# A hybrid block on one core: some of VectorE's products and sums given to GpSimd, with new ranks for the planner

## The chip, the core and the metric

The kernel runs on one NeuronCore of a Trainium2 chip. The time is the device time of one execution in microseconds (us); less is better. Engines are named as the profile names them: PE is TensorE (matmuls; PEld its weight loads), DVE is VectorE, ACT is ScalarE, POOL is GpSimd, SP is SyncE, which only issues DMAs. Each engine works through its own list of instructions in the order in which they stand; they wait for each other through semaphores.

## The reference

The input is x, 8 sequences of 256 tokens with 128 features, all in float32. Four layers are added to it one after the other, each on a layernorm of x:

```python
x = x + mamba(_layernorm(x))       # "m": a selective state space layer
x = x + moe(_layernorm(x))         # "p": 8 experts, two for each token
x = x + attention(_layernorm(x))   # "a": gated, with squared relu for the softmax
x = x + moe(_layernorm(x))         # "r": the same experts and weights again
```

In the first layer a projection gives 256 channels and a gate; a convolution over 4 tokens and a silu give h; delta = softplus(ts @ dt_w + dt_b); and for each of 256 channels and 16 states a recurrence runs over the 256 tokens: new = exp(A * delta) * old + delta * B * h, y = sum over the states of new * C, plus D * h. In an expert layer each token has a weight w_e for each of 8 experts (two are not zero), and the output is the sum over e of w_e * ((x @ w_up[e]) * silu(x @ w_gate[e])) @ w_down[e], with 352 inner features an expert.

## The kernel before

**Groups and lanes.** The 8 sequences are cut into four groups g of two, so a group has 512 tokens, which are the columns of nearly every tile (128 x 512). A group goes through lanes of work, each a Python generator: `prelude` (s: norm, projection, convolution, softplus), `recurrence` (m), `gating` (g), `ending` (f), `tail` (t), and `rest` (r: expert layer p, attention, expert layer r). `feeder` loads B and C rows and has ACT make the decays; `adder` issues the DMAs that sum the states' shares.

**Who sets the order.** A planner in the kernel, `Board` (L32 to L86), writes the order down when the program is built. Each lane offers its next operation with a cost in us; the planner takes the one that can start first by its own clock (`pick`, L73), with `RANKS` (L150) where several of one engine are near, and issues it. `SWITCH` is what it takes an ACT table load to cost. An engine's list is thus fixed before the kernel runs, and the chip follows it whether the costs were right or not. Where the planner thinks that PE will be idle for long before an operation, it puts dummy matmuls of 128 x 128 into its list (`fill`, L321 to L325, in `do` at L59 to L64), one for each 0.23 us of idle time as it sees it. They compute nothing that is used.

**The recurrence** (L724). 16 states by two channel halves are done in 16 steps for each group, 64 in all. A step is three instructions on DVE over 128 x 1024: a product (L744), a scan (L749) and a product (L753). All their operands are in SBUF. Then POOL issues a DMA (L716) that adds the step's result into an accumulator tile; five tiles `st0` to `st4` serve all.

**The softplus** (L607 to L635) is taken apart as max(v, 0) + log(1 + exp(-|v|)) with a correction. For each half c of the channels DVE subtracts the correction from dl (L624), later adds the logarithm to dl (L632), and multiplies dl by h to give du (L633). Decays are made from dl, the recurrence's first product reads du. In group 0 the two halves are separate steps; in later groups the correction (L622) is one instruction over both.

**An expert layer** (L945). The 8 x 352 inner features are 22 tiles of 128. For each tile: a gate product on PE (`gp`, L487), a silu on ACT (`sg`, L960), an up product on PE (`up`, L986, or L993 in four parts where a tile holds the end of one expert and the start of the next), a product on DVE (`it`, L1000, which reads `up` from PSUM), and two tiles later a down product on PE (`dn`, L1006). The token's weight is put into the input of `up`: a row of w_e is spread over the partitions by a DMA (`fetched`, L966) into a tile wb, and wb is multiplied by xT in place (`weighted`, L974 to L977, on DVE, both operands in SBUF). Of wb three tiles are held for each key, and expert e+2 is weighted when expert e has its last tile, two to three tiles ahead of its use. For layers in `SOON` the first expert's tile comes another way (L927 to L942).

**On POOL before the change** stand the L716 issues, the powers of the norms (L415), and the biases added to x (L494, 128 x 512), eight in all.

Of the kernel before, what the change touches and what calls it, by code (L numbers as in the profile page):

```python
# [10 lines left out]
ALU = mybir.AluOpType  # L11
# [20 lines left out]
class Board:  # L32
# [1 line left out]


    SWITCH = 1.3
    PATIENCE, LONG = 0, 0
    FILL = 0.23

    def given(self, op):  # L40
# [55 lines left out]
def kernel(  # L96
# [27 lines left out]
    nc = tc.nc  # L124
# [23 lines left out]
    BEHIND = 2  # L148

    RANKS = {  # L150
        "s": [0, 4, 4, 1.5], "m": [1.5, 2, 3, 3.5],
        "g": [4, 0, 3.5, 2], "t": [0, 3.5, 3.5, 0.5],
        "r": [2, 0.5, 2.5, 0.5], "f": [2.5, 1.5, 4, 0.5], "w": [0, 0, 0.3, 0], "feeder": 5, "adder": 0,
    }
    SOON = ("p0", "p1", "r0", "p3", "r3")
    SPLIT = ()
    ENDS = 2
    assert E * F % P == 0 and all(cut >= P or cut % CG == 0 for _, cut in OWNER)
# [36 lines left out]
    for name, src in (  # L195
# [10 lines left out]
        n = src.shape[0]  # L206
# [75 lines left out]
    def ring(pool, shape, tag, name, bufs=1):  # L282

        held = rings.setdefault((pool.name, tag), [])
        free = held[-bufs].used if len(held) >= bufs else 0.0
        h = Held(pool.tile(shape, FP, tag=tag, name=name, bufs=bufs), free)
        held.append(h)
        return h
# [40 lines left out]
    def dve(us, out, ins, issue):  # L329
        return Op("DVE", us, out, ins, issue, lag=0.06)  # L330
# [4 lines left out]
    def pool(us, out, ins, issue):  # L335
        return Op("POOL", us, out, ins, issue, lag=0.06)

    def load(us, out, ins, issue, queue="SP", take=0.1):
        return Op(queue, take, out, ins, issue, lag=us)

    def mm(n):
        return 0.005 + 0.00167 * n
# [4 lines left out]
    def dve_us(n):  # L347
        return 0.08 + 0.0012 * n
# [22 lines left out]
    for k in range(K):  # L371
# [6 lines left out]
    PARTS = [  # L378
        [(b, b + 1) for b in range(n)] if g in SPLIT else [(0, n)] for g, n in enumerate(SIZES)
    ]  # L380
# [137 lines left out]
    def prelude(g):  # L518

        GB = SIZES[g]  # L520
        G = GB * T
# [3 lines left out]
        xT = ring(norm, [P, G], "xTm", f"xT_m{g}")  # L525
# [4 lines left out]
        h = [ring(mam, [P, G], f"h{c}", f"h_{g}_{c}", bufs=2) for c in range(NI)]  # L530
# [52 lines left out]
        shut(ps)  # L583
        bc = Held(dram.tile([2 * N, G], FP, tag="bc", name=f"bc_{g}"))
        yield load(2.4, [bc], [ww], lambda: nc.sync.dma_start(bc.ap, xpj[R:XW, :]))

        dl = [ring(mam, [P, G], f"dl{c}", f"dl_{g}_{c}", bufs=2) for c in range(NI)]
# [22 lines left out]
        du = [ring(mam, [P, G], f"du{c}", f"du_{g}_{c}", bufs=2) for c in range(NI)]  # L612
# [6 lines left out]
        for (a, b), e, w in zip(parts, exs, wws):  # L619

            def lost():
                nc.vector.scalar_tensor_tensor(e.ap, w.ap, 1.0, e.ap, ALU.subtract, ALU.subtract)  # L622
                for c in range(a, b):
                    nc.vector.tensor_sub(dl[c].ap, dl[c].ap, e.ap[:, c - a, :])  # L624

            yield dve(2 * (b - a) * dve_us(G), [e] + dl[a:b], [w], lost)
        for (a, b), w in zip(parts, wws):
            yield act(act_us((b - a) * G), [w], [], lambda: nc.scalar.activation(w.ap, w.ap, AF.Ln, bias=zero), EXP)
        for (a, b), w in zip(parts, wws):
            for c in range(a, b):  # L630
                def step():
                    nc.vector.tensor_add(dl[c].ap, dl[c].ap, w.ap[:, c - a, :])  # L632
                    nc.vector.tensor_mul(du[c].ap, dl[c].ap, h[c].ap)  # L633

                yield dve(2 * dve_us(G), [dl[c], du[c]], [w, h[c]], step)  # L635
        if g > 0:

            for c in range(NI):
# [27 lines left out]
    def feeder():  # L666

        for g in range(NG):
# [6 lines left out]
            for q in range(N // NC):  # L675
# [4 lines left out]
                for tag, r0 in (("bt", q * NC), ("ct", N + q * NC)):  # L680
                    t = ring(scan, [P, NC, G], tag, f"{tag}_{g}_{q}", bufs=2)
                    yield load(4.0, [t], [bc], lambda: nc.sync.dma_start(
                        t.ap, bc.ap[r0 : r0 + NC, :].partition_broadcast(P)
                    ))
                    rows_at.append(t)
# [23 lines left out]
    def adder():  # L709

        while len(done & {f"f{g}" for g in range(NG)}) < NG:
            if not sums:
                yield None
                continue
            g, us, acc, st, into, of = sums.pop(0)
            yield load(us, [acc], [st], lambda: nc.gpsimd.dma_start(  # L716
                into, of, accum_op=ALU.add
            ), "POOL", 0.9)
            st.used = max(st.used, acc.ready)
            landed[g] = landed.get(g, 0) + 1  # L720
            if st is not acc:
                st.open = False
# [98 lines left out]
    def parted(g, tile):  # L821
        return tile, [Held(tile.ap[:, tokens(g, p)], tile.used) for p in range(len(PARTS[g]))]

    def whole(tile, parts):

        tile.ready = max(h.ready for h in parts)
        tile.used = max(h.used for h in parts)
        return tile
# [15 lines left out]
    def led_in(g, which, key, p, shared):  # L844
# [31 lines left out]
        if "we" not in shared:  # L876
# [8 lines left out]
            ]  # L885
            if f"{which}{g}" in SOON:
                shared["wb"] = parted(g, ring(
# [38 lines left out]

        if f"{which}{g}" not in SOON:  # L927
            return
# [16 lines left out]
    def moe(g, which, key, shared, ends):  # L945

        nm = f"{which}{g}"
        NT = SIZES[g] * TT
        G = NT * P
        xT, we = (whole(*shared[k]) for k in ("xT", "we"))  # L950
# [5 lines left out]
        def gate(i):  # L956
            gp = bank([P, G], f"gp_{nm}_{i}")
            yield pe(mm(G), [gp], [xT], product(gp.ap, [(wg_sb[:, i * P : (i + 1) * P], xT.ap)]))
            sg = ring(ffn, [P, G], f"sg{key}", f"sg_{nm}_{i}", bufs=SG)
            yield act(act_us(G), [sg], [gp], lambda: nc.scalar.activation(  # L960
                sg.ap, gp.ap, AF.Silu, bias=zero
            ), SILU)
            shut(gp)
            sgs[i] = sg
# [9 lines left out]
        def weighted(e):  # L974

            wb = wx[e]
            yield dve(dve_us(G), [wb], [xT], lambda: nc.vector.tensor_mul(wb.ap, wb.ap, xT.ap))  # L977

        def up(i, cols_of, sg, wa, wn, it, width):
# [49 lines left out]
        for i in range(LEAD):  # L1029
            yield from gate(i)  # L1030
        ahead = which + str(g) in SOON
        if not ahead:
# [3 lines left out]
        if not ahead:  # L1036
            yield from weighted(0)
        yield from weighted(1)

        dns = [  # L1040
# [4 lines left out]
        for i in range(NK - ENDS):  # L1045
            if i + LEAD < NK:
                yield from gate(i + LEAD)
            e, cut = OWNER[i]
            its[i] = tile_of(i)
            yield from up(i, everything, sgs.pop(i), wx[e], wx.get(e + 1), its[i], G)  # L1050
            if cut <= P:

                if e + WB < E:
                    yield from fetched(e + WB)
                if e + 2 < E:
                    yield from weighted(e + 2)
            if i >= BEHIND:
                it = its.pop(i - BEHIND)
                for p, dn in enumerate(dns):
                    yield from down(i - BEHIND, dn, it, tokens(g, p))  # L1060
# [179 lines left out]
    for g in range(NG):  # L1240
        waiting.append(Lane((RANKS["s"][g], g), prelude(g), [f"g{g - 1}"] * (g > 0) + [f"t{g - 2}"] * (g > 1)))
        waiting[-1].name = f"s{g}"
        waiting.append(Lane((RANKS["m"][g], g), recurrence(g), [f"s{g}"] + [f"m{g - 1}"] * (g > 0)))
        waiting[-1].name = f"m{g}"
        waiting.append(Lane((RANKS["g"][g], g), gating(g), [f"s{g}"] + [f"t{g - 1}"] * (g > 0)))
        waiting[-1].name = f"g{g}"
        waiting.append(Lane((RANKS["f"][g], g), ending(g), [f"m{g}"]))
        waiting[-1].name = f"f{g}"
        waiting[-1].patience = RANKS["w"][g]
        waiting.append(Lane((RANKS["t"][g], g), tail(g), [f"f{g}", f"g{g}"] + [f"t{g - 1}"] * (g > 0)))  # L1250
        waiting[-1].name = f"t{g}"
        waiting.append(Lane((RANKS["r"][g], g), rest(g), [f"t{g}"] + [f"r{g - 2}"] * (g > 1)))
        waiting[-1].name = f"r{g}"
# [57 lines left out]
```

## Time and profile before

| what | us |
|---|---|
| median of 3 runs (lowest to highest) | 759.33 (759.11 to 759.85) |
| the profiled execution's own time | 758.34 |
| its span, which all views below are of | 756.6 |
| end of the last L753 of groups 0, 1, 2, 3 in it | 121.78, 225.06, 376.33, 514.69 |
| DVE busy, all of it | 568.6 |
| ACT busy | 431.1 |
| POOL busy | 89.8 |

A span is cut into stages by these ends. A row of a group of instructions names line, engine, operation, output and inputs with their shapes, the count, the busy time in all, the mean in ns, and the idle time before them with what ended it. A matmul in float32 shows as two records. The row of dummy matmuls is L325. "Busy" PE is no measure of use, since the dummies count.

### The profile page before, as it was taken

The page shows a single profiled execution, that of the slowest core. Times are in us where ns is not written, and L with a number is a line of the kernel's source. Part 1 is how long each engine was busy: PE and PEld are TensorE (multiplying, and loading weights), DVE is VectorE, ACT ScalarE, POOL GpSimd, SP SyncE. Part 2 cuts the span into 40 slices and gives each one's busy share as a digit, 9 for nine tenths or more (in the row PEclk, how much of TensorE's full clock was granted, in tenths as well). Part 3 has the DMA queues.
Part 4 walks back from the last instruction along what each step waited for, and adds up shares of the span by engine and source line. Part 5 has one row for each costly group of instructions (what it writes and reads, how often), then busy time and mean ns, then how long its engine had stood idle before and what let it go on. Part 6 is the DMA issues. An engine that isn't in the chain of part 4 may idle for free.

```text
span 756.6 us, 8464 instructions
## 1 busy us (share of the span) xinstructions
PE 737.7 (98%) x3093; PEld 403.6 (53%) x3093; DVE 568.6 (75%) x824; ACT 431.1 (57%) x570; POOL 89.8 (12%) x110
## 2 busy tenths in 40 slices
PE   4999999999999999999999999999999999999997
PEld 3877996853446744434754533443555434644343
DVE  2599999999999999899999998995735334354332
ACT  5578333799947879977876677742252322432220
POOL 2021110311112210002120110011100001000000
PEclk9999999999999999999999999999999999999999
DMA  8719795399763345655774666745011200000110
GB/s 260 209 57 220 169 219 162 98 228 218 166 171 84 76 124 133 166 133 138 176 170 96 159 161 179 160 102 109 2 42 27 72 15 14 15 29 29 47 36 14
DMA packets 38903, 88.63 MB, mean 117 GB/s; under 512 B 4339, under 2 KB 14542, under 8 KB 38862
## 3 DMA queue, kind: packets, MB, share of 16 engines
q0 software_dynamic: 9312, 30.94, 22.8%
q1 hardware_dynamic: 20624, 41.54, 17.2%
q10 hardware_dynamic: 8926, 15.61, 6.8%
q8 instruction: 24, 0.39, 0.2%
q14 instruction: 17, 0.14, 0.0%
HBM read 55.71 MB, written 1.44 MB: 76 GB/s over the span
## 4 chain that ended last, share of the span: by engine, by line
PE 78%; DVE 15%; ACT 3%; issue 2%; ACTq 0%; DVEq 0%
PE gp_r L487 10%; PE dn_r L1006 10%; PE dn_p L1006 9%; PE gp_p L487 9%; PE up_r L986 7%; PE up_p L986 7%; DVE st L749 6%; PE up_r L993 3%; DVE st L744 3%; PE up_p L993 3%; DVE st L753 2%; PE av_a L1197 2%; PE tp_p L325 1%; PE xpj L325 1%; PE v_a L1131 1%
## 5 line engine op out<-in xcount | busy, mean ns | idle before, releaser
L749 DVE TENSOR_TENSOR_SCAN st<-decay,st 128x1024 f32<-128x1024 f32 x64 | 147.8, 2309 | 2.5
L960 ACT ACTIVATE sg_r<-gp_r,zero 128x512 f32<-128x512 f32 x88 | 59.9, 687 | 109.8 <-PE gp_r L487 88.7
L57 ACT ACT_TABLE_LOAD x89 | 114.2, 1283 | 8.0 <-PE dn_r L1006 3.6
L697 ACT ACTIVATE decay<-dl,zero,a_sb 128x510 f32<-128x510 f32 x128 | 96.2, 804 | 36.9 <-DVE st L749 35.7
L1000 DVE TENSOR_TENSOR it_r<-up_r,sg_r 128x512 f32<-128x512 f32 x88 | 60.4, 687 | 66.7 <-PE up_r L986 42.3
L960 ACT ACTIVATE sg_p<-gp_p,zero 128x512 f32<-128x512 f32 x88 | 59.3, 685 | 62.5 <-PE gp_p L487 46.6
L1000 DVE TENSOR_TENSOR it_p<-up_p,sg_p 128x512 f32<-128x512 f32 x88 | 60.3, 686 | 43.4 <-PE up_p L986 29.4
L1006 PE MATMUL dn_p<-it_p,wd_sb 128*128 128x512 f32 x176 | 91.2, 605 | 0.6 <-DVE it_p L1000 0.6
L1006 PE MATMUL dn_r<-it_r,wd_sb 128*128 128x512 f32 x176 | 90.5, 603 | 0.0
L716 POOL DMA_DIRECT2D st<-st x58 | 50.4, 874 | 334.2 <-DVE st L753 303.7
L487 PE MATMUL gp_r<-xT_r,wg_sb 128*128 128x512 f32 x176 | 90.0, 597 | 0.0
L487 PE MATMUL gp_p<-xT_p,wg_sb 128*128 128x512 f32 x176 | 89.0, 594 | 0.0
L744 DVE TENSOR_TENSOR st<-bt,du 128x1024 f32<-128x1024 f32 x64 | 78.8, 1231 | 0.0
L753 DVE TENSOR_TENSOR st<-st,ct 128x1024 f32<-128x1024 f32 x64 | 78.1, 1221 | 0.7
L986 PE MATMUL up_p<-wb_p,wu_sb 128*128 128x512 f32 x128 | 65.1, 594 | 0.0
L986 PE MATMUL up_r<-wb_r,wu_sb 128*128 128x512 f32 x128 | 64.9, 592 | 0.0
L1006 PEld LDWEIGHTS dn_p<-it_p,wd_sb 128*128 128x128 f32 x176 | 31.3, 189 | 47.1 <-issue 36.3
L487 PEld LDWEIGHTS gp_r<-xT_r,wg_sb 128*128 128x128 f32 x176 | 32.6, 190 | 42.7 <-issue 37.4
L1006 PEld LDWEIGHTS dn_r<-it_r,wd_sb 128*128 128x128 f32 x176 | 31.6, 190 | 44.3 <-issue 39.5
L487 PEld LDWEIGHTS gp_p<-xT_p,wg_sb 128*128 128x128 f32 x176 | 32.8, 190 | 41.2 <-issue 36.3
L325 PEld LDWEIGHTS y<-ident 128*128 128x128 f32 x428 | 48.0, 192 | 1.2 <-PE dt L487 0.8
L325 PE MATMUL y<-ident 128*128 128x128 f32 x428 | 48.2, 275 | 0.0
(217 smaller groups left out, 853.1 us busy)
## 6 DMA issues: line engine op xcount, KB each, us to landing
st<-st POOLq DMA_DIRECT2D x54, 512.0 KB, 6.4
bt<-bc SPq DMA_DIRECT2D x32, 512.0 KB, 6.0
ct<-bc SPq DMA_DIRECT2D x32, 512.0 KB, 4.5
wb_r<-wrow_r ACTq DMA_DIRECT2D x30, 256.0 KB, 3.8
wb_p<-wrow_p ACTq DMA_DIRECT2D x29, 256.0 KB, 3.9
st<-h POOLq DMA_DIRECT2D x6, 256.0 KB, 4.9
wg_sb<-in_L_ffn_w_gate_dram SPq DMA_DIRECT2D x2, 704.0 KB, 4.7
wu_sb<-in_L_ffn_w_up_dram SPq DMA_DIRECT2D x2, 704.0 KB
```

The lines of the kernel that those rows point to most:

```text
L57: self.load_tables(op.table)
L325: nc.tensor.matmul(ps[:, 0:n], lhsT=ident[:, 0:m], rhs=ident[:, 0:n], start=True, stop=True)
L487: nc.tensor.matmul(ps, lhsT=lhsT, rhs=rhs, start=(i == 0), stop=(i == len(terms) - 1))
L697: nc.scalar.activation(shaped[:, n, :, 1:], delta[c].ap.rearrange("p (b t) -> p b t", b=GB)[:, :, 1:], AF.Exp, bias=zero, scale=a_sb[:, c, ...
L716: yield load(us, [acc], [st], lambda: nc.gpsimd.dma_start(into, of, accum_op=ALU.add), "POOL", 0.9)
L744: yield dve(1.22, [st], [bt, du[c]], lambda: nc.vector.tensor_mul(st.ap, bt.ap, du[c].ap.unsqueeze(1).to_broadcast([P, NC, G])))
L749: yield dve(2.29, [st], [das[c]], lambda: nc.vector.tensor_tensor_scan(flat, das[c].ap.rearrange("p n t -> p (n t)"), flat, 0.0, ALU.mult, ...
L753: yield dve(1.22, [st], [ct], lambda: nc.vector.tensor_mul(st.ap, st.ap, ct.ap))
L960: yield act(act_us(G), [sg], [gp], lambda: nc.scalar.activation(sg.ap, gp.ap, AF.Silu, bias=zero), SILU)
L986: nc.tensor.matmul(ps.ap, lhsT=wu_sb[:, i * P : (i + 1) * P], rhs=wa.ap[:, cols_of], start=True, stop=True,)
L1000: yield dve(dve_us(width), [it], [ps, sg], lambda: nc.vector.tensor_mul(it.ap, ps.ap, sg.ap[:, cols_of]))
L1006: yield pe(mm(dn.ap.shape[1]), [dn], [it], lambda: nc.tensor.matmul(dn.ap, lhsT=wd_sb[:, i, :], rhs=it.ap[:, cols_of], start=(i == 0), sto ...
```

## The change

37 of the 59 weightings go from DVE to POOL: those of the expert layers named in the new list `SPARED`, p0, r0, p1, r1 and p2. In groups 1 to 3 the two subtractions and two additions to dl of the softplus go to POOL as well (12 instructions), the product du stays on DVE. The two halves are now separate steps for the planner. A cost for POOL is written down, `pool_us`: 1.33 for 512 columns by its formula. The ranks have other values, and `LONG` goes from 0 to 0.6: an ACT operation that would need another table is put back by `SWITCH` only if it could have started less than 0.6 us before. (The new key "late" is read nowhere.) With other costs and ranks the planner writes another order for every engine. The arithmetic and the number of instructions of each kind are the same, but for the dummy matmuls.

```diff
-    PATIENCE, LONG = 0, 0
+    PATIENCE, LONG = 0, 0.6
...
     RANKS = {
-        "s": [0, 4, 4, 1.5], "m": [1.5, 2, 3, 3.5],
-        "g": [4, 0, 3.5, 2], "t": [0, 3.5, 3.5, 0.5],
-        "r": [2, 0.5, 2.5, 0.5], "f": [2.5, 1.5, 4, 0.5], "w": [0, 0, 0.3, 0], "feeder": 5, "adder": 0,
+        "s": [3, 4, 4, 0.5], "m": [3.5, 2, 3, 3.5],
+        "g": [2, 0, 3.5, 2.5], "t": [4, 3, 3.5, 2],
+        "r": [2, 0.5, 2, 1], "f": [2, 1.5, 4, 0.5], "w": [0.3, 0, 2.3, 0], "late": 0, "feeder": 2.5, "adder": 0.5,
     }
     SOON = ("p0", "p1", "r0", "p3", "r3")
+
+    SPARED = ("p0", "r0", "p1", "r1", "p2")
...
+    def pool_us(n):
+        return 0.1 + 0.0024 * n
...
             def lost():
                 nc.vector.scalar_tensor_tensor(e.ap, w.ap, 1.0, e.ap, ALU.subtract, ALU.subtract)
-                for c in range(a, b):
-                    nc.vector.tensor_sub(dl[c].ap, dl[c].ap, e.ap[:, c - a, :])
-
-            yield dve(2 * (b - a) * dve_us(G), [e] + dl[a:b], [w], lost)
+
+            yield dve(dve_us((b - a) * G), [e], [w], lost)
+            for c in range(a, b):
+                if g > 0:
+                    yield pool(pool_us(G), [dl[c]], [e], lambda: nc.gpsimd.tensor_tensor(
+                        dl[c].ap, dl[c].ap, e.ap[:, c - a, :], ALU.subtract
+                    ))
+                else:
+                    yield dve(dve_us(G), [dl[c]], [e], lambda: nc.vector.tensor_sub(
+                        dl[c].ap, dl[c].ap, e.ap[:, c - a, :]
+                    ))
...
-                def step():
-                    nc.vector.tensor_add(dl[c].ap, dl[c].ap, w.ap[:, c - a, :])
-                    nc.vector.tensor_mul(du[c].ap, dl[c].ap, h[c].ap)
-
-                yield dve(2 * dve_us(G), [dl[c], du[c]], [w, h[c]], step)
+                if g > 0:
+                    yield pool(pool_us(G), [dl[c]], [w], lambda: nc.gpsimd.tensor_tensor(
+                        dl[c].ap, dl[c].ap, w.ap[:, c - a, :], ALU.add
+                    ))
+                else:
+                    yield dve(dve_us(G), [dl[c]], [w], lambda: nc.vector.tensor_add(
+                        dl[c].ap, dl[c].ap, w.ap[:, c - a, :]
+                    ))
+                yield dve(dve_us(G), [du[c]], [dl[c], h[c]], lambda: nc.vector.tensor_mul(
+                    du[c].ap, dl[c].ap, h[c].ap
+                ))
...
         def weighted(e):
 
             wb = wx[e]
+            if nm in SPARED:
+                yield pool(pool_us(G), [wb], [xT], lambda: nc.gpsimd.tensor_tensor(
+                    wb.ap, wb.ap, xT.ap, ALU.mult
+                ))
+                return
             yield dve(dve_us(G), [wb], [xT], lambda: nc.vector.tensor_mul(wb.ap, wb.ap, xT.ap))
```

In the changed kernel the weightings on POOL are L996, the subtractions L632, the additions L644, the product du L651, the dummy matmuls L327, the adding DMAs L734, and a step of the recurrence L762, L767, L771.

## The prediction

> **What bounds the kernel now.** I read the busy rows of the page first, then the dummy matmuls by stage, then DVE's and POOL's timelines where both work.
>
> ```profile
> PE 737.7 (98%) x3093; PEld 403.6 (53%) x3093; DVE 568.6 (75%) x824; ACT 431.1 (57%) x570; POOL 89.8 (12%) x110
> DVE  2599999999999999899999998995735334354332
> POOL 2021110311112210002120110011100001000000
> ```
>
> DVE is full until about slice 27 of 40 and then a third busy; POOL is nearly free. That PE is 98% busy says little: dummies count. The windows of busy time, cut at the end of group 0's recurrence and at that of the last, and the same windows of the dummies' line L325:
>
> ```profile
> 0.00:129.00 129.00, 116.62 (x823) 97.88 (x824) 103.69 (x109) 70.42 (x100) 20.24 (x39) 1.00 0.71 184
> 129.00:511.00 382.00, 380.56 (x1456) 193.56 (x1456) 359.10 (x490) 289.12 (x361) 59.37 (x61) 1.00 0.61 148
> 511.00:756.60 245.60, 240.47 (x817) 112.16 (x815) 105.81 (x227) 71.60 (x110) 10.23 (x10) 1.00 0.13 34
> ```
>
> ```profile
> 0.00:129.00 129.00, 85.99 (x746) 85.65 (x746) 1.00 0.71 184
> 129.00:166.00 37.00, 17.35 (x147) 17.27 (x148) 1.00 0.65 158
> 166.00:511.00 345.00, 25.48 (x205) 24.85 (x204) 1.00 0.61 147
> 511.00:756.60 245.60, 4.38 (x32) 4.20 (x32) 1.00 0.13 34
> ```
>
> After the length of the window the columns of the first three rows are PE, PEld, DVE, ACT, POOL, clock, DMA share, GB/s; those of the other four PE and PEld on L325. **Stage A** (to 129) is DVE's: two thirds of PE there are dummies, and the chain of waits goes L744, L749, L753 over and over. **Stage C** (from 511) is PE's: almost no dummies, DVE at 43%. **Stage B** is shared: PE has 352 records of dummies, and DVE is busy 359.1 of 382. PE waits for nothing longer than 0.6 us there, so every lost PE microsecond of B is a dummy that the planner wrote for a wait that it foresaw. The chain shows their pace:
>
> ```profile
> 132.31 6.47 PE tp_p L325 x58
> ```
>
> 58 records are 29 dummies, 0.223 us each.
>
> **What leaves DVE, and what POOL takes.** The groups of instructions, by form:
>
> ```profile
> L977 DVE TENSOR_TENSOR wb_p<-wb_p,xT_p 128x512 f32<-128x512 f32 x29 | 19.8, 682 | 1.0 <-DMA wb_p<-wrow_p 1.0
> L632 DVE TENSOR_TENSOR dl<-dl,ww 128x512 f32<-128x512 f32 x8 | 5.5, 682 | 0.0
> L494 POOL TENSOR_TENSOR x<-x,b_first 128x512 f32<-128x512 f32 x4 | 5.5, 1364 | 22.7 <-DMA b_first<-in_L_attn_a_out_b_dram 16.3 <-ACT xn_m L437 6.5
> ```
>
> An operation costs DVE 0.687 us (L977, L624 and L632 together), and POOL 1.27 where it is undisturbed (L494's shortest and median). 37 weightings and 12 sums make 49: 33.7 us off DVE, 62 us on POOL. Of these, the 4 sums of group 1 lie in A; B loses 35 weightings and 8 sums from DVE (43 x 0.687 = 29.5), and POOL gets 45 there, since two of p2's weightings stood in C before.
>
> **What it costs DVE all the same.** Here the rows speak against the change; the timeline of DVE and POOL (start, length):
>
> ```profile
> 143.77 1.26 POOL L494 TENSOR_TENSOR x<-x,b_first 128x512 f32<-128x512 f32 x1 [0.71 <-ACT xn_m L437]
> ...
> 144.13 1.99 DVE L744 TENSOR_TENSOR st<-bt,du 128x1024 f32<-128x1024 f32 x1
> ...
> 238.38 3.32 POOL L494 TENSOR_TENSOR x<-x,b_back 128x512 f32<-128x512 f32 x1 [2.69 <-DVE xn_a L422]
> ...
> 240.48 0.68 DVE L512 TENSOR_TENSOR x<-x,pb_m 128x512 f32<-128x512 f32 x1
> 241.08 2.76 DVE L749 TENSOR_TENSOR_SCAN st<-decay,st 128x1024 f32<-128x1024 f32 x1
> ```
>
> L744 takes 1.22 else: it stood for 0.77 us behind the bias. In the second case POOL waits through L753 and L744, gets in when L512 runs (which reads PSUM), and holds up the scan, 2.29 else, by 0.47. The other L494 beside a busy DVE delayed a scan by 0.89, a pair product by 0.98 and a weighting by 0.85; beside L1000, with one operand in PSUM, nobody lost. Mean of the five: 0.79 us, more than the 0.687 saved. The Trainium skill ("SBUF — State Buffer", Who interferes with whom) has the rule: a VectorE instruction with two SBUF inputs and a GpSimd instruction that reads SBUF exclude each other, and whoever comes second blocks fully. By the rule alone each move would cost DVE up to 1.27, 45 x 1.27 = 57 us in B, and B would be far over 382. The rows give less, as part of POOL's time falls beside products from PSUM.
>
> For the changed kernel I estimate the stolen time s of one POOL operation so. The recurrence's instructions take (147.8 + 78.8 + 78.1) x 48/64 = 228 us of B, with pair products and du some 65% of the time: POOL then waits, and mostly gets in beside an it product, which the changed order puts between nearly any two instructions of a step: 0.5. In the other 35% it comes in the middle: 0.9. s = 0.65 x 0.5 + 0.35 x 0.9 = 0.64, between ends of 0 (all beside PSUM products or idle time) and 0.98. So B asks of DVE 329.6 + 45 x 0.64 = 358.4, what it asked before.
>
> **PE's list.** The order of the built program has 564 dummies before and 497 after: up to group 0's last product 361 and 349, in B 187 and 132, in C 16 and 16. Real matmuls are the same. So PE's list for B is shorter by 55 x 0.223 = 12.3 us: 369.7. That is what the planner believes, which costs a POOL operation at 1.33 and knows of no stolen time. Is DVE ready for that? It idles 6% of B before, for want of `up` results; but between 170 and 200 it idled 0.8% and from 200 to 300 5%, and PE stood still in neither. If it needs 3%, B is 358.4 / 0.97 = 369.5, and the plan holds; if it keeps its 6%, B is 381.3, nothing gained. I take the middle, 375.4: -6.6.
>
> **Stage A.** Four sums leave DVE, -2.75. Nothing but port-holding instructions runs there, so each POOL sum steals what the scan at 45.77 lost, 0.89: +3.6. The two du products now wait on DVE for POOL, whose queue has two L734 issues (0.87 each) in between, and behind du stand the steps of group 0, which are the path. I add 0.7. Net +1.5; ends -2.75 (stolen time nil) and +4.4 (du waits for two whole POOL operations, 2.5, besides). The dummies before `y` that go (12) are beside DVE's path: nothing.
>
> **The rest.** A weighting is due two to three tiles ahead, each tile three matmuls of 0.86: 5 to 8 us of cover for a POOL operation of 1.3 to 3.3; uncovered it would stop PE, 1 to 2 us each time. The L734 issues queue behind weightings and the reverse (an L734 waits for its L767 and L771, and the weighting behind it too); a landed sum frees a state tile, but DVE's L744 shows no idle time for one now, and a delay of 1.3 on 6.4 us to landing leaves the three spare tiles enough at a step each 8 us. SP's loads follow L744 and L753 and move with them. ACT has 89 table switches by the plan in both orders, 0. Prelude 2 stands at the end of recurrence 1: four POOL operations in row (5.1 us) ahead of du, foreseen by the planner at nearly their true cost, and beside it products. C: PE's list is the same, 0.
>
> **Sum.** 1.5 - 6.6 = -5.1: span 756.6 to 751.5, own time 758.34 to 753.2. The median of the runs lies 1.0 above the profiled one's time, so 754.2; I say 754.
>
> **The rivals.**
> - *The plan holds* (s under 0.3, DVE has room everywhere): -12.3 and -2.75, 744. For it: in B DVE's planned load is 329.6 of 369.7. Against it: all five L494 that met a busy DVE before 511 cost it 0.47 or more. 0.10.
> - *Even* (757.8 to 760.8): where dummies were, PE now stands and waits; DVE keeps its 6%, s near 0.64, B 381, A +1.5, near 760. 0.17.
> - *Slower by the port*: s is the measured mean 0.79 and DVE keeps its 6% idle: (329.6 + 35.6) / 0.94 = 388.5, +6.5, and A +1.5: 767. It decides from s = 0.66 with 6% idle, from 0.91 with 3%. The place is B, above all where the orders crowd moved operations: five in a stretch of 17 us of PE work at the second half of recurrence 2. For it: each row above. Against it: L1023 between the steps' instructions, and that PE reads a product two tiles later, so that half a microsecond on DVE needn't reach it. 0.28.
> - *The likeliest*: half of the dummies' time is gained, 754 (749 to 757.8). 0.45.
>
> A difference under 0.2% (1.5 us) is no difference here. Faster 0.10 + 0.45 = 0.55, within 0.17, slower 0.28. The range is 746 to 767: it leaves out most of the first rival (0.06) and what lies over the third one's price (0.12).
>
> **What would show it.** Right: L767 and L762 with a mean above 2.31 and 1.23, the sum of their excess and that of L771 over 64 steps at 20 to 35 us; L996 mostly between 1.27 and 3.3; recurrence 0 ending at 123.3, the last at about 510; dummies at 0.88 of before. Wrong: PE waits for it products (`dn` <- `it`) that sum to over 12 us, or `up` <- wb L996 in rows of 1 us or more (then POOL's queue was mis-sized); L767 at 2.31 (then the port was).

## The result and the profile after

| what | before | after |
|---|---|---|
| median of 4 runs each (lowest to highest), us | 759.49 (759.11 to 759.85) | 778.28 (777.57 to 779.12) |
| the profiled execution's own time, its span | 758.34, 756.6 | 779.12, 777.3 |
| end of the last product by C of groups 0, 1, 2, 3 | 121.78, 225.06, 376.33, 514.69 | 125.24, 238.75, 399.66, 536.69 |

The changed kernel is slower: the ratio of the times is 1.0248, with a 95% interval of 1.023 to 1.0266. The predicted 754.0 and the range's upper end, 767, both lie below the measured time.

The busy rows of the page of the changed kernel, with three rows of its 40 slices:

```profile
PE 739.5 (95%) x2959; PEld 393.3 (51%) x2959; DVE 578.8 (74%) x775; ACT 431.2 (55%) x570; POOL 164.0 (21%) x159
...
DVE  2499998899998899899998896997644444263332
...
POOL 2031510242224241632231223214010000000000
PEclk9999998999999999999998998999999999999999
```

DVE has 49 instructions fewer (824 to 775) and is busy for longer, 568.6 to 578.8 us. POOL went from 89.8 to 164.0. And the row PEclk, all nines before, has three eights: PE's granted clock fell somewhere. The windows, cut as the prediction cut those of before (7.2 us after the end of group 0's recurrence, 3.7 before that of the last), with the same columns (PE, PEld, DVE, ACT, POOL, clock, DMA share, GB/s):

```profile
0.00:132.50 132.50, 115.69 (x780) 94.56 (x780) 102.85 (x103) 68.64 (x99) 30.07 (x42) 0.97 0.69 179
132.50:533.00 400.50, 384.32 (x1367) 186.94 (x1367) 370.89 (x449) 291.51 (x363) 121.07 (x105) 0.97 0.58 142
533.00:777.30 244.30, 239.49 (x815) 111.78 (x813) 105.09 (x225) 71.01 (x109) 12.86 (x12) 1.00 0.12 34
```

Stage A grew by 3.5 us (129 to 132.5), B by 18.5 (382 to 400.5), C shrank by 1.3. In B, DVE should have fallen from 359.1 by 29.5 to 329.6; it rose to 370.9. So 41 us came back, and the groups of instructions by form show where. Before, then after, three rows of the recurrence, and after them the weightings on POOL (columns: count, busy time in all, mean in ns, idle time before):

```profile
L749 DVE TENSOR_TENSOR_SCAN st<-decay,st 128x1024 f32<-128x1024 f32 x64 | 147.8, 2309 | 2.5
...
L744 DVE TENSOR_TENSOR st<-bt,du 128x1024 f32<-128x1024 f32 x64 | 78.8, 1231 | 0.0
L753 DVE TENSOR_TENSOR st<-st,ct 128x1024 f32<-128x1024 f32 x64 | 78.1, 1221 | 0.7
```

```profile
L767 DVE TENSOR_TENSOR_SCAN st<-decay,st 128x1024 f32<-128x1024 f32 x64 | 156.6, 2447 | 5.3 <-ACT decay L715 1.9
...
L762 DVE TENSOR_TENSOR st<-bt,du 128x1024 f32<-128x1024 f32 x64 | 97.0, 1516 | 0.0
...
L771 DVE TENSOR_TENSOR st<-st,ct 128x1024 f32<-128x1024 f32 x64 | 81.1, 1267 | 0.8
...
L996 POOL TENSOR_TENSOR wb_p<-wb_p,xT_p 128x512 f32<-128x512 f32 x22 | 34.0, 1576 | 13.4 <-DMA wb_p<-wrow_p 13.4
...
L996 POOL TENSOR_TENSOR wb_r<-wb_r,xT_r 128x512 f32<-128x512 f32 x15 | 24.3, 1619 | 7.5 <-DMA wb_r<-wrow_r 7.5
```

The same instructions on the same data take 8.8 + 18.2 + 3.0 = 30 us more, most of it in the first product, L762. Counting every DVE instruction for what it took beyond the median of its own form (where that is over 0.1 us), I get from the trace 0.9 us in A and 3.1 in B before, and 5.1 and 39.0 after. I call this "stretched time" below, and give it for A and B together where no stage is named: 4.0 before, 44.1 after.

The waits of PE after the change, longest sums first (columns: us in all, times, longest):

```profile
PE cols_ps L356 <- DMA out_w_sb<-in_L_attn_a_out_w_dram: 6.7, 1, 6.7
PE dn_p L1029 <- DVE it_p L1023: 4.5, 4, 1.6
PE tp_m L457 <- ACT xn_m L442: 4.3, 2, 2.8
PE conv L492 <- ACT padded L541: 4.2, 2, 2.9
PE y L492 <- DVE st L771: 4.2, 1, 4.2
PE up_p L1009 <- POOL wb_p L996: 3.0, 1, 3.0
PE weT_ps_r L1039 <- DVE we_r L939: 2.8, 1, 2.8
```

The first and the third stood there before (6.6 and 4.3). The other five are new or grown. Four of them hold a single wait of 2.8 to 4.2 us that the planner did not foresee: no dummies fill it, or too few (two ahead of `conv`); `dn_p` has four waits of at most 1.6. What such a wait looks like, and what it brings after it, is in the timeline of PE, DVE and POOL around 200 us (start, length):

```profile
196.70 0.88 POOL L734 DMA_DIRECT2D st<-st  x1 [5.50 <-PE dn_p L1029]
...
196.92 3.06 DVE L762 TENSOR_TENSOR st<-bt,du 128x1024 f32<-128x1024 f32 x1
...
197.30 1.58 POOL L996 TENSOR_TENSOR wb_p<-wb_p,xT_p 128x512 f32<-128x512 f32 x1
...
198.00 0.61 PE L327 MATMUL conv<-ident 128*128 128x128 f32 x4
...
201.51 4.11 PE L492 MATMUL conv<-padded,taps_sb 128*128 128x512 f32 x5 [2.90 <-ACT padded L541]
```

L762 takes 3.06 us; its median is 1.22. It begins after POOL's L734 and before the weighting L996, and ends 1.1 us after the weighting's end: 1.84 us lost to an operation that POOL does in 1.27 undisturbed. PE then stands for 2.90 us and, when it starts again, needs 4.11 us for five records of matmuls over 512 columns, which take 0.43 each at full clock. The windows of PE over that place (busy time, then granted clock, DMA share, GB/s):

```profile
196.50:201.64 5.14, 2.24 (x9) 1.00 0.71 148
201.64:205.06 3.42, 3.42 (x5) 0.50 0.42 165
205.06:208.00 2.94, 2.94 (x8) 1.00 1.00 259
```

Half the clock for 3.42 us. After the change there are five such stretches, at 119.72, 143.62, 201.64, 413.27 and 471.3 us, of 3.41 or 6.83 us, 27.3 us in all, ahead of one at the very end; before, there is only the one at the end, in the last three microseconds. (The record of the clock begins at 15 to 17 us.) Four of the five belong to the waits for `y`, `conv`, `weT_ps_r` and `up_p` above: three begin in the last 0.9 us of the wait, that of `conv` 0.13 us after it. The one at 143.62 follows none.

A balance of PE's list between the last product by C of the first recurrence and that of the last (my sums from the trace) says where the 18.5 us of B sit: dummies -12.0, as the plan had it (374 records to 266); PE's idle time +14.4 (1.8 to 16.2); half clock +10.1 (PE was busy for 20.1 us in it). That gives 12.5 of the 18.5; the other 6.0 are not placed by this sum. In A such a sum decides nothing, since DVE is the path there.

### The profile page after: what moved, and what is told of

It reads as the page before. It is cut to its first block, busy times and chain, and to the rows that moved or that the text cites. A ratio compares the mean times of both kernels' runs of the same rounds, so it can differ in the third digit from the quotient of the medians.

```text
span 777.3 us, 8223 instructions
## 1 busy us (share of the span) xinstructions
PE 739.5 (95%) x2959; PEld 393.3 (51%) x2959; DVE 578.8 (74%) x775; ACT 431.2 (55%) x570; POOL 164.0 (21%) x159
## 3 DMA queue, kind: packets, MB, share of 16 engines
q1 hardware_dynamic: 20624, 41.54, 17.1%
## 4 chain that ended last, share of the span: by engine, by line
PE 60%; DVE 28%; issue 4%; ACT 3%; POOL 1%; DMA 1%; ACTq 0%; DVEq 0%; POOLq 0%
DVE st L767 9%; PE dn_r L1029 8%; PE gp_r L492 8%; PE dn_p L1029 7%; PE gp_p L492 6%; DVE st L762 6%; PE up_r L1009 6%; PE up_p L1009 5%; DVE st L771 4%; PE up_r L1016 2%; PE up_p L1016 2%; PE y L492 2%; PE av_a L1220 1%; DVE it_p L1023 1%; PE conv L492 1%
## 5 line engine op out<-in xcount | busy, mean ns | idle before, releaser
L767 DVE TENSOR_TENSOR_SCAN st<-decay,st 128x1024 f32<-128x1024 f32 x64 | 156.6, 2447 | 5.3 <-ACT decay L715 1.9
L734 POOL DMA_DIRECT2D st<-st x58 | 50.8, 886 | 238.8 <-DVE st L771 190.6
L762 DVE TENSOR_TENSOR st<-bt,du 128x1024 f32<-128x1024 f32 x64 | 97.0, 1516 | 0.0
L492 PE MATMUL gp_r<-xT_r,wg_sb 128*128 128x512 f32 x176 | 92.0, 610 | 0.0
L771 DVE TENSOR_TENSOR st<-st,ct 128x1024 f32<-128x1024 f32 x64 | 81.1, 1267 | 0.8
L327 PEld LDWEIGHTS y<-ident 128*128 128x128 f32 x404 | 45.3, 192 | 1.5 <-PE dt L492 0.8
L327 PE MATMUL y<-ident 128*128 128x128 f32 x404 | 45.5, 275 | 0.0
```

Of the source, the lines that this page charges most:

```text
L327: nc.tensor.matmul(ps[:, 0:n], lhsT=ident[:, 0:m], rhs=ident[:, 0:n], start=True, stop=True)
L492: nc.tensor.matmul(ps, lhsT=lhsT, rhs=rhs, start=(i == 0), stop=(i == len(terms) - 1))
L734: yield load(us, [acc], [st], lambda: nc.gpsimd.dma_start(into, of, accum_op=ALU.add), "POOL", 0.9)
L762: yield dve(1.22, [st], [bt, du[c]], lambda: nc.vector.tensor_mul(st.ap, bt.ap, du[c].ap.unsqueeze(1).to_broadcast([P, NC, G])))
L767: yield dve(2.29, [st], [das[c]], lambda: nc.vector.tensor_tensor_scan(flat, das[c].ap.rearrange("p n t -> p (n t)"), flat, 0.0, ALU.mult, ...
L771: yield dve(1.22, [st], [ct], lambda: nc.vector.tensor_mul(st.ap, st.ap, ct.ap))
```

## The experiments

My theory after the result: POOL's operations, while they read SBUF, hold up DVE's (the port), and PE's new waits and its half clock follow from that. The rivals: the new ranks and order are worse in themselves; POOL's queue is late with the weightings. All medians are set against runs of the kernel before on the same chip.

**1. The same order, everything on DVE.** The planner plans as for the changed kernel, so each engine's list is the same, but the 49 operations are issued to DVE at their places.

```diff
-                yield pool(pool_us(G), [wb], [xT], lambda: nc.gpsimd.tensor_tensor(
+                yield pool(pool_us(G), [wb], [xT], lambda: nc.vector.tensor_tensor(
```

(and so for the 12 sums)

> The order that the planner wrote for the changed kernel, each of the 49 moved operations at its place, but issued on VectorE. Port theory: the 40 us by which DVE instructions are stretched in the changed kernel (39.0 in stage B, 5.1 in A) go, 33.7 us of work come back; with them the sum of PE's four waits of about 3 us and its time at half clock shrink. 765 to 774, stretched time under 5 us. Order theory (the new ranks are what is slower): 778 as the changed kernel. Queue theory (weightings come late on POOL, behind the adding DMAs): 765 to 772 as well, PE's wait for a weighting gone.

Measured: 756.44, ratio 0.9965 (0.9953 to 0.9977). The very plan that takes 778.3 takes 756.4 when DVE does the work itself. The order is not what makes the kernel slower; I had not expected it to be better than the kernel before. The wait for the weighting is there all the same:

```profile
PE up_p L1009 <- DVE wb_p L996: 3.6, 1, 3.6
```

So that wait belongs to the order (the row's DMA lands late there), and not to POOL's queue.

**2. The new ranks and LONG without the moves**, planned anew with everything on DVE.

```diff
-    SPARED = ("p0", "r0", "p1", "r1", "p2")
+    SPARED = ()
...
-                if g > 0:
+                if False:
```

> New ranks and LONG, all 49 operations back on VectorE and known to the planner as such. Its list for PE has 599 dummies, 35 more than before (7.8 us). Port theory: no stretched instructions, no waits that the plan did not foresee, so before plus the dummies, about 767, and granted clock near 1.0. Order theory: 775 or more.

Measured: 765.94, ratio 1.0092 (1.0077 to 1.0107). In a plan that does not take DVE to be relieved, the new ranks cost 6.7 us.

**3. The moves with the old ranks.**

```diff
-    PATIENCE, LONG = 0, 0.6
+    PATIENCE, LONG = 0, 0
...
-        "s": [3, 4, 4, 0.5], "m": [3.5, 2, 3, 3.5],
+        "s": [0, 4, 4, 1.5], "m": [1.5, 2, 3, 3.5],
...
```

> The 49 moves with the ranks and LONG of before. 584 dummies, 20 more than before (4.5 us). Port theory: stretched DVE time of 30 to 45 us again, unforeseen waits of PE and clock drops: 775 to 790. Order theory: 764 or less.

Measured: 787.9, ratio 1.038 (1.0364 to 1.0395), with 37.0 us of stretched time in B. Under either set of ranks the moves, each time with the order that the planner writes for them, cost time: 28.7 us under the old, 12.3 under the new (778.3 - 765.9).

**4. POOL writes without reading.** Each moved operation becomes three memsets of the same tile, so this kernel leaves out the weightings and the sums. POOL's queue is as full as in the changed kernel (about 1.8 us for the three, where the product takes 1.57 at the median), every semaphore stays, only POOL's reading of SBUF is gone.

```diff
+    def blind(t):
+        for v in (0.03, 0.02, 0.01):
+            nc.gpsimd.memset(t, v)
...
-                yield pool(pool_us(G), [wb], [xT], lambda: nc.gpsimd.tensor_tensor(
-                    wb.ap, wb.ap, xT.ap, ALU.mult
-                ))
+                yield pool(pool_us(G), [wb], [xT], lambda: blind(wb.ap))
```

> The changed kernel's order to the letter, but each of the 49 POOL operations is replaced by three memsets of the same tile (the sums of delta and the weighting are left out, so the output isn't the reference's): POOL writes SBUF and reads nothing. Port theory: a two-operand DVE instruction competes only for the read side, so the stretched time falls from 44 us to under 8, PE's unforeseen waits and clock drops go, and what the plan promised comes: 744 to 752. Queue or order theory: 772 or more, since queue, order and waits on POOL are the same.

Measured: 751.87, ratio 0.9902 (0.9886 to 0.9919). The groups by form of this kernel:

```profile
L767 DVE TENSOR_TENSOR_SCAN st<-decay,st 128x1024 f32<-128x1024 f32 x64 | 148.3, 2318 | 5.5 <-ACT decay L715 2.2
...
L771 DVE TENSOR_TENSOR st<-st,ct 128x1024 f32<-128x1024 f32 x64 | 79.8, 1247 | 0.8
L762 DVE TENSOR_TENSOR st<-bt,du 128x1024 f32<-128x1024 f32 x64 | 78.7, 1230 | 0.0
...
L348 POOL MEMSET wb_p<- 128x512 f32 x66 | 38.7, 588 | 15.1 <-DMA wb_p<-wrow_p 11.2 <-PE gp_p L496 1.4
```

L762 is back at 1230 ns and the stretched time at 5.8 us, with POOL no less busy than in the changed kernel (172.5 us for 164.0). So POOL's reading costs 778.3 - 751.9 = 26.4 us, the half clock that follows from it included, and the same order without it is 7.4 us faster than the kernel before. (Two stretches of half clock, 6.8 us, are left here; one comes after a wait of 3.8 us for the first weighting of p2.) The Trainium skill ("SBUF — State Buffer", Who interferes with whom) says that a DVE instruction with two inputs in SBUF contends with a GpSimd instruction that reads SBUF and not with one that only writes it: this pair of runs agrees, 44.1 us of stretched time against 5.8.

**5 and 6. One part alone, in the same order.** In the fifth the 12 sums go back to DVE, in the sixth the 37 weightings, by the edit of the first.

> The changed kernel's order to the letter, the 12 sums of softplus back on VectorE, the 37 weightings on POOL. Port theory, by the stretched time of the changed kernel (5.1 us in stage A, where only sums are on POOL; 39.0 in B, of which the sums of groups 2 and 3 share some 5): A loses 3 us of it, B keeps about 35. 771 to 775. If instead the sums were the cause through the recurrence's start (du waits for POOL): under 765.

> The reverse: the same order, the 37 weightings on VectorE, the 12 sums on POOL. Port theory: stretched time of 5 in A and some 5 in B; the same-order kernel (756.4) plus what the sums steal, 758 to 763. If the sums were the cause: 770 or more.

Measured: 770.53 with the weightings on POOL, ratio 1.0149 (1.0133 to 1.0164), and 760.49 with the sums on POOL, 1.0016 (1.0007 to 1.0025). Against the first experiment's 756.4 the weightings cost 14.1 us, the sums 4.1, both together 21.8. The fifth kernel's DVE is busy 580.0 us, no less than the changed kernel's 578.8, and it is 7.7 us faster. Its recurrence 0 ends at 122.0 us, 3.2 earlier, and it stands at half clock for 17.1 us in place of 27.3. So the total on DVE doesn't set the time.

**7. Keep PE's clock up.** 60 dummies more, written in ahead of the four operations that the half clock follows (20, 13, 13 and 14).

```diff
+    def warm(h, n):
...
+        for _ in range(n):
+            nc.tensor.matmul(ps[:, 0:k], lhsT=ident[:, 0:m], rhs=ident[:, 0:k], start=True, stop=True)
```

> The changed kernel with 60 more dummy matmuls (13.4 us of PE time), put just ahead of the four operations for which PE waits 2.8 to 4.2 us: the first y product of group 0, the first convolution of group 2, the transposed weights of r1, the first up product of p2. They fill the waits and shorten none. Clock theory (after such a wait PE's clock stands at half for 3.4 to 6.8 us, 24 us in all in four places, and the matmuls there take double): the drops vanish, 767 to 772. If the half clock costs nothing since PE would wait anyway: 777 to 779; if the dummies push the work: over 780.

Measured: 770.25, ratio 1.0139 (1.0124 to 1.0154), mean clock 1.0 where the changed kernel has 0.981. The stretched time stays (45.8 us), and B falls from 400.5 to 393.1. So 8.0 of the 19 us are the clock's. The first experiment shows the same within one kernel: of its 16 executions, the nine with a mean clock of 0.995 took 754.5 to 756.7 us, the seven with 0.989 to 0.993 took 756.8 to 759.4. The Trainium skill ("TensorE: Matmul & The Clock Gate", Part 1) has the rule: after a window of about 3.4 us with PE idle the clock is halved, until about as long a window of work has passed. Stretches of 3.41 and 6.83 us, one and two such windows, fit. Waits shorter than such a window were enough here, of 2.8 to 3.0 us in the list above and of 2.06 in experiment 1, so the measurement differs from the rule in this; what exactly brings the clock down is left open.

**8. A memset between.** Six L762 and one other instruction were held up by 1.74 to 1.84 us each, 12.7 us together, as in the timeline above. Does POOL's next operation take hold of the port while it still waits behind the L734? Then a small memset ahead of it would shorten these.

```diff
+    scrap = const.tile([P, 1], FP, name="scrap")
...
-                yield pool(pool_us(G), [wb], [xT], lambda: nc.gpsimd.tensor_tensor(
+                yield pool(pool_us(G), [wb], [xT], lambda: (nc.gpsimd.memset(scrap, 0.0), nc.gpsimd.tensor_tensor(
```

> The changed kernel with a memset of a 128 x 1 scratch tile (it reads nothing) ahead of each of the 49 POOL operations. Seven DVE instructions in the changed kernel start 0.2 us after an adding DMA's issue on POOL and 0.3 us ahead of the POOL product behind it, and still stand until that product ends, 1.83 us. If the product takes the read side when it comes into the queue behind the issue: the memset keeps it off until the issue is done, DVE comes first at these seven, stretched time falls from 44 to about 32, and the time to 768 to 774. If the read side is taken at the product's own start: 44 again, 777 to 780.

Measured: 776.1, ratio 1.0227 (1.0201 to 1.0253). The held-up L762 still take 3.0 to 3.1 us each and the stretched time is 46.2 us. So the memset did not keep POOL off, and the first of the two cases foreseen did not come. The 2 us go with less half clock in this execution (17.1 us in place of 27.3).

**9. A drain between.** The same with `nc.gpsimd.drain()` in place of the memset, so that POOL begins nothing before all that it has issued is over.

> The changed kernel with a drain on POOL ahead of each of the 49 operations, so that it cannot begin in any part before the DMA issue or product ahead of it on POOL has ended. Theory of the early start (parts of POOL that have no work in the adding DMA's issue go on at once to the product behind it and hold the read side all that time; the memset did not stop that): the seven DVE instructions that stood 1.83 us come first, their stretched time is nearly gone, stretched time 44 to some 30 us, 768 to 775. If the read side is held for another reason: the seven still at 3.0 us, 776 or more.

Measured: 806.54, ratio 1.0613 (1.0581 to 1.0645). The time was missed by 30 us, since a drain behind an adding DMA mostly stood for 6 to 9 us, and the operation after it began only 0.2 to 0.6 us after that DMA had landed: the weightings came late. PE's waits in this kernel:

```profile
PE up_p L1016 <- POOL wb_p L996: 12.9, 5, 3.8
PE y L492 <- DVE st L771: 9.7, 1, 9.7
...
PE up_p L1009 <- POOL wb_p L996: 5.9, 1, 5.9
```

But the stretched time fell from 44.1 to 19.0 us, the seven cases are gone, and nothing is held up by more than 1.21. That fits the first expectation, that an operation standing ready behind an issue takes hold early. It does not show it: the drains also put all of POOL's work at other times. Why seven instructions lost more than POOL's own time stays open.

**10. The first experiment with 24 dummies more**, nine ahead of `y` of group 0 and 15 ahead of the late `up` of p2, where it lost clock.

> The same order on VectorE (756.4 before the change to it) with 24 dummies in two of PE's waits: 9 ahead of the first y product of group 0, 15 ahead of the first up product of p2, whose waits were 2.1 and 3.6 us and each followed by 3.4 us at half clock. Clock theory: some 3 us less, 752.5 to 755.5. If half clock costs nothing there: 756.

Measured: 754.39, ratio 0.9938 (0.9925 to 0.9952). It beats both kernels: the new order with nothing moved to POOL and two unforeseen waits covered (PE's wait at that `up` falls from 3.6 to 0.8 us).

**11. The kernel before with fewer dummies.** The prediction took a dummy in B for time that can be had. Here the kernel before writes them only beyond 0.8 us of foreseen idle time.

```diff
-            for _ in range(int((idle - 0.3) / self.FILL)):
+            for _ in range(int((idle - 0.8) / self.FILL)):
```

> The kernel before with its own order, and each group of dummies shorter by about two (from 0.8 us of foreseen idle time on instead of 0.3): 475 dummies for 564, in stages B and C 139 for 203, 14.3 us. If the dummies of B fill waits that are really there, these come back as waits: 757 to 760 (or more, should the clock drop). If they are spare, as the sum of the prediction took them: 745 to 750. The same-order kernel, 67 dummies shorter than before and 3 us faster, lies nearer to the first.

Measured: 759.16, ratio 1.0001 (0.9993 to 1.001). 89 dummies less (564 to 475), 64 of them, 14.3 us by the duration of one, after stage A, and nothing gained: PE's busy time falls from 737.7 to 723.4 us in the same span, and its idle time grows by as much. A shorter list of PE is no gain where the dummies stand in true waits.

## Why the prediction was wrong

- **The mechanism was right and ranked too low.** The third rival, slower by the port, is what happened; the prediction placed it at 767 with 0.28. The sign that it chose could not tell the two apart: L767 and L762 above 2.31 and 1.23 with 20 to 35 us of excess stood there as a sign of being right, and 30 us came. But 45 x 0.64 = 28.8 and 45 x 0.79 = 35.6 lie too near each other for such a range.
- **The step that failed: s.** The rows of before gave a mean of 0.79 us stolen for each POOL operation, and the prediction argued it down to 0.64, since POOL would mostly get in beside an `it` product. Measured in B: (39.0 - 3.1) / 45 = 0.80, the mean of the five rows. In A: (5.1 - 0.9) / 4 = 1.05, against 0.89 taken. Since one move saves 0.687, the sign of what DVE gets from a move hung on it: at 0.64 it gains 0.05, at 0.80 it loses 0.11. With 0.80 and everything else as it stood, B would be 382.9 in place of 375.4, and the time 762: dearer than before, but not yet 778. The rest lies in three more terms: DVE's idle time, the clock and stage A.
- **Cases that no row of before had.** The seven of about 1.8 us, where the largest loss in a row of before is 0.98, and POOL operations in a row, which DVE did not get between. The timeline of DVE and POOL at 331 us:

```profile
329.81 2.79 POOL L644 TENSOR_TENSOR dl<-dl,ww 128x512 f32<-128x512 f32 x2
...
331.42 4.18 DVE L651 TENSOR_TENSOR du<-dl,h 128x512 f32<-128x512 f32 x1 [1.92 <-POOL dl L644]
...
332.26 2.78 POOL L996 TENSOR_TENSOR wb_p<-wb_p,xT_p 128x512 f32<-128x512 f32 x2
```

 A du product of 0.69 us lasted 4.18, through the second L644 and both weightings, and had waited 1.92 for the first sum before that. This is prelude 3 in the second half of recurrence 2, the place that the third rival named. Ten instructions (the seven, this product, a scan of 4.72 and a pair product of 2.52) hold 20.7 of the 39.0 us in B. One of the seven, `we_r` at 411.95, is what PE waits for at `weT_ps_r`.
- **PE's list.** "So PE's list for B is shorter by 12.3 us" was true as a count (-12.0) and wrong as a gain. Experiment 11 shows that the dummies of before stand in real waits; even with almost no port loss (experiment 4) A and B together got only 6 us shorter in the trace.
- **Idle DVE.** The prediction took the middle between 3% and 6%. By its own formula, 329.6 + 45 x 0.80 = 365.6 at 6% idle is 388.9 us for B. DVE had 370.9 to do in that window (3.5 of the 5 us more are one product and one scan that fall inside this cut), at 6% 394.6, and idled 7.4%: 400.5. With PE's clock kept up (experiment 7) it has 369.8 to do and idles 5.9% of 393.1. So DVE kept its 6%, and the rest of its idle time is PE's half clock come back to it.
- **The clock was not in the sum at all.** Unforeseen waits were priced at their length. Four of them cost 8.0 us on top (experiment 7). Without that the time is 770, 3 us from the third rival's price. This nearness is in part luck: in experiment 7, B costs 11.1 us and A 3.7 more than before, where that rival had 6.5 and 1.5, and C gives back 2.5.
- **Stage A**: +1.5 predicted, +3.5 measured. DVE is busy for 1.5 us longer up to the end of recurrence 0 (4.2 stolen, 2.75 saved) and idle for 2.0 longer, in waits ahead of the du products: 0.85 for `rstd_m` from POOL, 0.7 and 0.4 for `ex` and `padded` from ACT. Experiment 4 has the same three waits, so they are not the port's. The du products, for which 0.7 was set aside, waited for nothing, and PE's half clock at `y` costs nothing here: experiment 7 ends recurrence 0 at 125.5, no earlier than 125.24. **The weightings' cover** held but for one wait of 3.0 us, which the order has without POOL too. **C** at 0: -1.3. **ACT's tables**: 89 in both, as said.
- **A sign badly chosen.** "PE waits for it products that sum to over 12 us" was to show the loss. They sum to 4.5; the lateness came out in single waits elsewhere (`conv`, `y`, `weT_ps_r`), because whatever DVE does next is late, not only the products between the steps.

## What to carry to other kernels

Before giving GpSimd an elementwise operation with SBUF operands, count what it takes from VectorE where that works on two SBUF operands: here 0.80 us for every 0.687 saved. Where the trace has the very conflict, take its mean as it stands, and look for cases outside its rows in the changed order, instead of arguing the number down. Dummies that a planner writes are a record of its foreseen waits and no reserve, and a wait of some three microseconds without them can be paid again in PE's clock: here four cost 8.0 us more than their length.

## What was not expected of the hardware

- DVE can lose more than POOL's operation lasts: 1.84 us to one that lasted 1.58 in the timeline and stood behind a DMA issue (0.88) on POOL; and a DVE instruction that comes between POOL operations in a row is held to their end, 4.18 us for 0.69 and, at 161 us behind a bias and a weighting, 4.72 for 2.29.
- POOL's memsets of the same tiles, about 1.8 us at each place, cost DVE next to nothing (5.8 us of stretched time, 4.0 before).
- A drain on POOL behind an adding DMA mostly stood for 6 to 9 us, until that DMA had landed.
- PE's clock fell to half after a wait of 2.06 us in experiment 1 (before `y`) and at 143.62 us of the changed kernel after no wait: PE was busy for 3.72 of the 3.80 us before, in part with router matmuls of 8 columns and dummies of 32. After a wait of 2.28 us in experiment 11 (before `conv`, at 49 us) it did not fall. The length of a wait alone doesn't tell.
